# A two-layer cross-attention kernel: the first step of a turn's image probabilities set behind the next scores, and four row subtractions set one stop earlier

## The chip, the cores and the metric

The kernel runs on one core of one Trainium2 chip. The metric is the device time of one execution in microseconds (us), as the median of several runs. The engines are called as the profile calls them: PE is TensorE, the matrix engine (PEld is its weight load); DVE is VectorE, ACT is ScalarE, POOL is GpSimd; SPq is the queue on SyncE that issues nearly all DMAs.

## The reference

Two cross-attention layers run one after the other on `x` of shape (4, 512, 320), with 20 heads of width 16 and a context `ctx` of (4, 1024, 512). The last 4 tokens of the context are image tokens in layer 0; in layer 1 the first 77 are text and all others image tokens. Everything is float32.

```python
# layer 0
probs_t = softmax(q k_t^T * 0.25)                  # over 1020 text tokens
text_out = probs_t @ v_t
qsem = l2norm(probs_t @ text_ehs)                  # [.., 512] for each head and row
sem  = qsem @ l2norm(ip_ehs)^T
probs_ip = softmax(q k_ip^T * 0.25 + 0.5 * sem)    # over 4 image tokens
probs_ip = probs_ip * spatial_mask
x = (text_out + probs_ip @ v_ip) @ W_out + b_out + x
# layer 1
out_text = softmax(q k^T * 0.25) @ v               # over 77 tokens
out_ip   = softmax(q k_ip^T * 0.25) @ v_ip         # over the other 947
x = (out_text + out_ip) @ Wo.T + bo + x
```

## The kernel before

The rows of `x` are cut into 16 **turns** of 128 rows (4 batches, 4 turns each). Each turn has 5 **groups** of 4 heads, so the main loop runs over 80 groups `gi`. A group has two **units** (`i` = 0, 1) of two heads, and a unit four parts (`part0` to `part3`), which multiply probabilities with blocks of the context on PE (tiles `b` in PSUM, operands `xv`, `xs`, `xv_t`, `xs_t`; two of the products run on sums of blocks in the manner of Strassen and Winograd). After each part comes a **stop**; stops of a group are numbered `k` = 0 to 7. The stops hold the rest of the work:

- `item()` (stop 0 to 7, first thing) takes one piece from the queues `sub`, `late` and `proj`, in this order: a transpose for layer 1, small steps that finish layer 0's turn and start layer 1's, or a projection of the next batch.
- `fill0(gi + 1, k)` (stops 0 and 1) makes the next group's scores: 32 PE matmuls into two `sc` tiles of PSUM; ACT copies both to `e` (L490), DVE reduces both for the row maximum (`m<-sc`). There are two `sc` buffers in all, so the second fill's matmuls need the first fill's copies and reductions done. Layer 1's tiles `mx` and `ex` use the same two buffers.
- `l1_step()` (stops 2, 4, 5 and mostly 6) is a step of layer 1: maxima (`mx`, `m<-mx`, `nmz`), exponentials (`ex`, L551), and at stop 4 the values' product `pv`, which ACT copies to `pc` (L567). Its normalisation (`den`: a shuffle and a reciprocal on DVE, two products on POOL) is put at the end of `late` and mostly runs at stop 5.
- `max0(gi + 1)` (stop 2) transposes the row maxima, writes them to DRAM (`zd`) and reads them back broadcast over partitions (`bc`, 256 KB, L737).
- `end_stop(k)` (last thing of a stop) takes from `ew` the four pieces that `max0` put there. Each piece (`do_exp`) adds `bc`, the negated maximum of the row, to one `e` tile on DVE and takes ACT's exponential of it (L748). For half 0 the add is one instruction of 128x1024, and POOL then subtracts one block from another (L750); for half 1 it is a 128x768 add and a 128x256 `scalar_tensor_tensor` with `drop`. The order is unit 0 half 0, unit 0 half 1, unit 1 half 0, unit 1 half 1; below they are the first to fourth subtraction.

On POOL a unit also has its sum of blocks `s2` (L824), `e("11") + s2` (L843, needed by `part1`) and `e("12") - s2` (L845, needed by `part2`). `part0` ends with the DVE add `c<-b,p`, which needs ACT's copy `p` (L842); ACT then squares `c` (L828). `part1` lets DVE copy `p5` out of its tile (a row `p<-b`), and `part2` ends with the DVE adds `c<-b,u` and `c<-b,p`; the second of them reads the tile into which `part3` multiplies next.

After a turn's last group `finish(turn)` runs. `norms()` makes, on DVE, the reciprocal `r` of the sums, the squared norms `n` (five small instructions), `o` and `sem`, and on ACT `rn` (Ln and Exp). `exps()` is four small DVE instructions (`sem<-sem,rn`, `pe<-sem,ips`, `mx<-pe`, `pe<-pe,mx`) and an exponential on ACT (L910). It goes to `late` with five further steps, so that `item()` runs it at stop 0 of the next turn's first group, ahead of that stop's fill.

PE's and DVE's instructions are kept in the order in which the program records them. ACT's, POOL's and the DMA queues' are placed by the framework's scheduler.

Of the kernel before, what the change touches and what calls it, by code (L numbers as in the profile page):

```python
# [33 lines left out]
TURNS = [(b, s) for b in range(B) for s in range(ST)]  # L34
# [21 lines left out]
def xattn_pair(ctx_stack: ExitStack, tc: tile.TileContext, a: dict, out: bass.AP):  # L56
# [19 lines left out]
    def mm(out, lhsT, rhs, start, stop, on=False):  # L76
        tc.keep_in_program_order(nc.tensor.matmul(out, lhsT=lhsT, rhs=rhs, start=start, stop=stop, skip_group_check=on))  # L77
# [13 lines left out]
    def tr(out, in_, ident):  # L91
        tc.keep_in_program_order(nc.tensor.transpose(out, in_, ident))  # L92
# [11 lines left out]
    def tp(name):  # L104
        turn_of[0] += 1
        if tail[0]:
            return ps_tp.tile([P, 512], F32, tag="tp", name=name)
        if idle[0] and turn_of[0] % 4:
            return ps_qs.tile([P, 512], F32, tag=f"qs{turn_of[0] % 4 - 1}", name=name)
        return ps_tp.tile([P, 512], F32, tag="tp", name=name)  # L110
# [39 lines left out]
    def load_x(b, s, ns, pl, tag):  # L150
        t = pl.tile([P, ns, C], F32, tag=tag, name=f"{tag}_{b}_{s}")
        nc.sync.dma_start(t, a["x"][b, s * P : (s + ns) * P, :].rearrange("(t p) c -> p t c", p=P))
        return t
# [89 lines left out]
    def zero_below(t):  # L243
        nc.gpsimd.memset(t[64:, NC - 1, :], 0.0)
        return t
# [210 lines left out]
    late = deque()  # L456
# [3 lines left out]
    hold = [0]  # L460
    ready = {}
    pend = []
    ew = deque()

    def load_quad(l, z, turn, g):

        s = TURNS[turn][1]
        q = z.q1d[turn] if l else z.q0d[:, s * P : (s + 1) * P]
        k = buffer(l, turn, g)
        for r in range(4):  # L470
            c = 64 * g + D * r
            nc.sync.dma_start(qq[l][k][32 * r : 32 * r + D, :], q[c : c + D, :])
            nc.sync.dma_start(kq[l][k][32 * r : 32 * r + D, :], z.kd[l][c : c + D, :])
# [4 lines left out]
    def fill(c, m, name):  # L478


        ps = [ps_sc.tile([P, 2, 512], F32, tag="sc", name=f"sc{name}_{c}_{i}") for i in range(2)]
        for j in range(TH):
            t = (TH * c + j) * P
            for r in range(4):
                mm(ps[r // 2][:, r % 2, j * P : (j + 1) * P], kq[0][0][32 * r : 32 * r + D, t : t + P],
                   qq[0][0][32 * r : 32 * r + D, :], True, True)
        e = [ep.tile([P, 2, TH, P], F32, tag="e0", name=f"e{name}_{c}_{i}") for i in range(2)]

        for i in range(2):
            nc.scalar.copy(e[i].rearrange("p h t s -> p (h t s)"), ps[i].rearrange("p h n -> p (h n)"))  # L490
            j = 1 - i
            vec.tensor_reduce(m[:, c, 2 * j : 2 * j + 2, :],
                              ps[j][:, :, 0 : (TH - c) * P].rearrange("p h (t s) -> p h s t", s=P), AX.X, ALU.max)
        return e
# [185 lines left out]
    def l1_step():  # L680
        if stops[0] < hold[0]:
            return
        if l1:
            l1.popleft()()
        elif pend:
            pend.pop()()
# [14 lines left out]
    def fill0(gi, c):  # L701
        if gi >= len(G):
            return
        name = f"0_{gi}"
        if c == 0:
            ms[gi] = big.tile([P, 2, 4, P], F32, tag="m0", name=f"m{name}")
        e = fill(c, ms[gi], name)
        for i in range(2):
            es[gi, i, c] = e[i]
        if c:  # L710

            m = ms[gi]
            vec.tensor_tensor(m[:, 0], m[:, 0], m[:, 1], ALU.max)
            for i in range(2):
                x = m[:, 0, 2 * i : 2 * i + 2, :]
                vec.scalar_tensor_tensor(x, x, drop[:, 0:1], e[i][:, :, TH - 1, :], ALU.add, ALU.max)
            if gi + 1 < len(G):
                turn, g = G[gi + 1]
                load_quad(0, zs[TURNS[turn][0]], turn, g)
# [149 lines left out]
    def finish(turn):  # L869
        b, s = TURNS[turn]  # L870
        w, z, name = state.pop(turn), zs[b], f"0_{turn}"

        def small(tag, shape):
            return (st2 if tag in ("pT", "oT") else big).tile(shape, F32, tag=tag, name=f"{tag}_{name}")

        def wide(t, n=NIP):
            return t.unsqueeze(2).to_broadcast([P, H, n])

        z.xr[turn] = xr = load_x(b, s, 1, st3, "xr")
        nc.gpsimd.tensor_tensor(xr, xr, bo[0].unsqueeze(1).to_broadcast([P, 1, C]), ALU.add)  # L880
        pv, ss, ips = w["pv"], w["ss"], w["ips"]
        r = small("r", [P, H])
        o = small("o", [P, H, D])
        sem = small("sem", [P, H, NIP])
        n2 = small("n2", [P, H])
        rn = small("rn", [P, H])
        pe = small("pe", [P, H, NIP])
        mx = small("mx", [P, H])
        sums = small("sums", [P, H])
        re = small("re", [P, H])  # L890


        def norms():

            vec.reciprocal(r, pv[:, :, V0W - 1])
            vec.tensor_tensor(n2, ss[:, :, 0], ss[:, :, 1], ALU.add)
            vec.tensor_tensor(n2, n2, r, ALU.mult)
            vec.tensor_tensor(n2, n2, r, ALU.mult)
            vec.tensor_scalar(n2, n2, EPS2, None, ALU.max)
            nc.scalar.activation(rn, n2, AF.Ln)  # L900
            nc.scalar.activation(rn, rn, AF.Exp, scale=-0.5)
            vec.tensor_tensor(o, pv[:, :, 0:D], wide(r, D), ALU.mult)
            vec.tensor_tensor(sem, pv[:, :, D : D + NIP], wide(r), ALU.mult)

        def exps():
            vec.tensor_tensor(sem, sem, wide(rn), ALU.mult)
            vec.scalar_tensor_tensor(pe, sem, SEM_SCALE, ips, ALU.mult, ALU.add)
            vec.tensor_reduce(mx, pe, AX.X, ALU.max)
            vec.tensor_tensor(pe, pe, wide(mx), ALU.subtract)
            nc.scalar.activation(pe, pe, AF.Exp)  # L910

        def shares():
            vec.tensor_reduce(sums, pe, AX.X, ALU.add)
            vec.reciprocal(re, sums)
            vec.tensor_scalar(re, re, spat[:, s : s + 1], None, ALU.mult)
            vec.tensor_tensor(pe, pe, wide(re), ALU.mult)

        of2, box = o.rearrange("p h d -> p (h d)"), {}

        def turn_ip():  # L920
            pt = tp(f"pt_p_{name}")
            tr(pt[: H * NIP, 0:P], pe.rearrange("p h n -> p (h n)"), ident)
            box["pT"] = small("pT", [H * NIP, P])
            vec.tensor_copy(box["pT"], pt[: H * NIP, 0:P])

        def add_ip():
            pt = tp(f"pt_ip_{name}")
            mm(pt[:, 0:C], box["pT"], z.vip, True, True)
            vec.tensor_tensor(of2, pt[:, 0:C], of2, ALU.add)

        def turn_out():
            pt = tp(f"pt_o_{name}")
            for c, (c0, n) in enumerate(CK):
                tr(pt[:n, c * P : (c + 1) * P], of2[:, c0 : c0 + n], ident)
            box["oT"] = zero_below(small("oT", [P, NC, P]))
            vec.tensor_copy(box["oT"][:, 0:2].rearrange("p c s -> p (c s)"), pt[:, 0 : 2 * P])
            vec.tensor_copy(box["oT"][:64, 2, :], pt[:64, 2 * P : 3 * P])

        def multiply():
            pt = tp(f"pt_y_{name}")  # L940
            for c in range(NC):
                mm(pt[:, 0:C], box["oT"][:, c, :], wo0[:, c, :], c == 0, c == NC - 1)
            vec.tensor_tensor(xr[:, 0, :], pt[:, 0:C], xr[:, 0, :], ALU.add)
            layer1(turn)

        norms()
        late.extend([exps, shares, turn_ip, add_ip, turn_out, multiply])


    z, (turns, keys0, last_k, v0, vip, keys1, v1, q0) = projections(0)  # L950
# [55 lines left out]

    def end_stop(k):
        stops[0] += 1
        for _ in range({5: 2, 6: 1, 7: 1}.get(k, 0)):
            if ew:  # L1010
                ew.popleft()()

    def item():
        for q in (late,) if tail[0] and l1 else (sub, late, proj):
            if q:
                q.popleft()()
                break

    def stop(gi, k):

        item()
        if k < 2:
            fill0(gi + 1, k)
        if k in (2, 4, 5) or k == 6 and gi < len(G) - 2 or ending[0] and k < 2:
            l1_step()
        if k == 2:
            max0(gi + 1)
        end_stop(k)
# [65 lines left out]
```

## Time and profile before

| | |
|---|---|
| median of 3 runs | 3616.77 us (3614.4 to 3620.53) |
| the profiled execution's own time | 3614.53 us |
| its span, first to last instruction | 3612.8 us |
| mean granted PE clock | 0.973 of full speed |
| PE busy | 3496.2 us (97%) |
| PE's weight loads busy | 2787.8 us (77%) |
| DVE busy | 2101.1 us (58%) |
| ACT busy | 1471.5 us (41%) |
| POOL busy | 1021.5 us (28%) |

A row of the timeline reads: start in us from the span's start, duration in us, engine, source line, operation, tiles written and read, shape, count, and in brackets the idle time of the engine just before and what ended it. Rows of one kind that follow each other are merged. Most of DVE's instructions and all of PE's are recorded by helpers, so that they all stand at L87 and L77; the tiles tell them apart. An engine that is idle beside a busy PE costs nothing; what costs time is PE's own waiting, and PE's time at half clock.

### The profile page before, as it was taken

Reading aid. Unit: us, or ns where it says so; the run is one execution under the profiler, and the core shown is the slowest. Engines: PE = TensorE matmul, PEld = TensorE weight load, DVE = VectorE, ACT = ScalarE, POOL = GpSimd, SP = SyncE. Lnnn points to the kernel's source line nnn. Section 1 sums busy time; section 2 is a strip of 40 time slices with the busy share of each in tenths; the row PEclk is TensorE's granted clock in tenths of the full one; section 3 lists DMA queues with packets and bytes.
Section 4 is the critical chain, followed back from the end, with each engine's and each line's share of the span. In section 5 each row is a group of like instructions: output and inputs, shape, how many; then the busy total and the mean of one; then the engine's idle time right before and its main releaser. Section 6 shows DMA issues by size and latency. Waiting matters only on the chain.

```text
span 3612.8 us, 74199 instructions
## 1 busy us (share of the span) xinstructions
PE 3496.2 (97%) x29060; PEld 2787.8 (77%) x29060; DVE 2101.1 (58%) x3814; ACT 1471.5 (41%) x2807; POOL 1021.5 (28%) x1050
## 2 busy tenths in 40 slices
PE   7999999999999999999999999999999999999989
PEld 6777777777788777877777788777778777777766
DVE  2344555666655655566664655656666666666644
ACT  1333344444443443444443443444444444444422
POOL 2322222323332222233222232222323323332310
PEclk9999999999999999999999999999999999999976
DMA  6454332222344243222234434222232222222211
GB/s 210 107 130 118 96 67 41 44 42 55 81 98 114 56 103 97 56 52 41 58 78 112 97 83 102 57 60 44 48 84 49 46 45 52 43 47 42 47 31 32
DMA packets 700571, 258.76 MB, mean 72 GB/s; under 512 B 567952, under 2 KB 673904, under 8 KB 700224
## 3 DMA queue, kind: packets, MB, share of 16 engines
q1 hardware_dynamic: 699184, 250.42, 30.9%
q8 instruction: 232, 3.80, 0.5%
q0 software_dynamic: 864, 3.41, 0.4%
q14 instruction: 115, 0.94, 0.1%
q10 hardware_dynamic: 176, 0.20, 0.0%
HBM read 213.51 MB, written 40.33 MB: 70 GB/s over the span
## 4 chain that ended last, share of the span: by engine, by line
PE 85%; DVE 7%; ACT 3%; issue 2%; DMA 1%; SPq 1%; POOL 0%; POOLq 0%; ACTq 0%; DVEq 0%
PE b L77 50%; PE ex L77 6%; PE pv L77 5%; PE mx L77 4%; PE sc L77 4%; PE pt_k L77 4%; PE pt_v L77 4%; DVE e L87 4%; PE pt_y L77 2%; PE pt_q L77 2%; ACT e L490 2%; DVE m L87 1%; PE mx L92 1%; ACT e L748 1%; ACT junk L828 1%
## 5 line engine op out<-in xcount | busy, mean ns | idle before, releaser
L77 PE MATMUL b<-xv_t,e 128*128 128x277 f32 x2560 | 662.3, 401 | 1.7 <-DVE c L87 1.6
L77 PE MATMUL b<-xv,e 128*128 128x277 f32 (+1 forms) x2560 | 649.4, 406 | 2.8 <-ACT e L748 2.8
L77 PEld LDWEIGHTS b<-xv,e 128*128 128x128 f32 x2560 | 478.7, 189 | 134.7 <-ACT e L748 3.4
L77 PEld LDWEIGHTS b<-xv_t,e 128*128 128x128 f32 x2560 | 476.2, 191 | 108.7 <-DVE c L87 4.0
L748 ACT ACTIVATE e<-e 128x1024 f32<-128x1024 f32 x320 | 338.2, 1057 | 462.9 <-DVE e L87 462.8
L843 POOL TENSOR_TENSOR e<-e,s 128x512 f32<-128x512 f32 x160 | 224.0, 1400 | 982.5 <-PE b L77 982.4
L87 DVE TENSOR_REDUCE m<-mx 128x2 f32<-128x870 f32 (+3 forms) x345 | 366.7, 1066 | 115.4 <-PE ex L77 92.2
L87 DVE TENSOR_REDUCE m<-sc 128x256 f32<-128x1024 f32 (+1 forms) x320 | 343.3, 1088 | 135.4 <-PE sc L77 119.1
L551 ACT ACTIVATE e<-ex 128x1024 f32<-128x1024 f32 x320 | 325.7, 1019 | 209.0 <-PE ex L77 208.0
L490 ACT COPY e<-sc 128x1024 f32<-128x1024 f32 x320 | 320.4, 1010 | 177.6 <-PE sc L77 150.5
L77 PE MATMUL mx<-kq,qq 16*128 16x512 f32 x1280 | 380.2, 668 | 6.3 <-DMA qq<-q1d 4.0
L77 PE MATMUL ex<-qa,kq 19*128 19x128 f32 x5120 | 382.2, 291 | 3.8 <-DVE qa L87 3.1
L87 DVE TENSOR_TENSOR e<-e,bc 128x1024 f32<-128x1024 f32 x320 | 369.8, 1177 | 2.2 <-DMA bc<-zd 2.2
L750 POOL TENSOR_TENSOR e<-e 128x512 f32<-128x512 f32 x160 | 205.7, 1285 | 571.2 <-ACT e L748 567.1
L87 DVE TENSOR_TENSOR c<-b,p 128x256 f32<-128x256 f32 x320 | 134.1, 419 | 389.2 <-PE b L77 341.0
L828 ACT ACTIVATE junk<-c 128x256 f32<-128x256 f32 x480 | 198.6, 414 | 395.7 <-DVE c L87 391.2
L77 PEld LDWEIGHTS ex<-qa,kq 19*128 19x128 f32 x5120 | 324.5, 194 | 16.9 <-issue 6.3
L77 PE MATMUL b<-xs,e 128*128 128x256 f32 x1280 | 335.1, 407 | 0.0
L77 PE MATMUL b<-xs_t,e 128*128 128x256 f32 x1280 | 320.0, 393 | 4.3 <-POOL e L843 4.3
L77 PE MATMUL b<-xs_t,s 128*128 128x256 f32 x1280 | 302.7, 379 | 0.0
L77 PEld LDWEIGHTS b<-xs,e 128*128 128x128 f32 x1280 | 240.7, 198 | 48.8 <-issue 2.1
L77 PEld LDWEIGHTS b<-xs_t,e 128*128 128x128 f32 x1280 | 231.5, 190 | 55.4 <-issue 13.9
(190 smaller groups left out, 4173.6 us busy)
## 6 DMA issues: line engine op xcount, KB each, us to landing
kq<-kd SPq DMA_DIRECT2D x640, 64.0 KB
v1q<-v1d SPq DMA_DIRECT2D x80, 373.5 KB
bc<-zd SPq DMA_DIRECT2D x80, 256.0 KB
xv<-v0d SPq DMA_DIRECT2D x480, 42.0 KB
xv_t<-v0d SPq DMA_DIRECT2D x320, 42.0 KB
L_xattn_W_k<-in_L_xattn_W_k_dram SPq DMA_DIRECT2D x13, 640.0 KB
L_xattn_Wv_ip<-in_L_xattn_Wv_ip_dram SPq DMA_DIRECT2D x13, 640.0 KB
raw<-in_ctx_dram SPq DMA_DIRECT2D x32, 256.0 KB
```

Of the source, the lines that this page charges most:

```text
L77: tc.keep_in_program_order(nc.tensor.matmul(out, lhsT=lhsT, rhs=rhs, start=start, stop=stop, skip_group_check=on))
L87: return lambda *args, **kw: keep(getattr(self.engine, name)(*args, **kw))
L92: tc.keep_in_program_order(nc.tensor.transpose(out, in_, ident))
L490: nc.scalar.copy(e[i].rearrange("p h t s -> p (h t s)"), ps[i].rearrange("p h n -> p (h n)"))
L551: nc.scalar.activation(e.rearrange("p i j s -> p (i j s)"), ps.rearrange("p i n -> p (i n)"), AF.Exp)
L748: nc.scalar.activation(flat, flat, AF.Exp)
L750: nc.gpsimd.tensor_tensor(e[:, 1], e[:, 1], e[:, 0], ALU.subtract)
L828: nc.scalar.activation(junk, x, AF.Square, accum_out=self.w["ss"][:, self.h + r, k : k + 1])
L843: nc.gpsimd.tensor_tensor(self.e("11"), self.e("11"), self.s2, ALU.add)
```

## The change

Two edits:

1. `exps()` no longer goes to `late`. It is kept in a queue `after`, and at stop 0 of the next turn's first group it runs behind `fill0` in place of that stop's `item()`; the five further steps are put into `late` when it has run. The last turn is as before.
2. `end_stop` takes the four subtractions at stops 4 (one), 5 (two) and 6 (one), where it took them at stops 5 (two), 6 (one) and 7 (one).

```diff
+    after = deque()
     ew = deque()
...
         norms()
-        late.extend([exps, shares, turn_ip, add_ip, turn_out, multiply])
+
+        def exps_and_on():
+            exps()
+            late.extend([shares, turn_ip, add_ip, turn_out, multiply])
+
+        (after if turn + 1 < len(TURNS) else late).append(exps_and_on)
...
     def end_stop(k):
         stops[0] += 1
-        for _ in range({5: 2, 6: 1, 7: 1}.get(k, 0)):
+        for _ in range({4: 1, 5: 2, 6: 1}.get(k, 0)):
             if ew:
                 ew.popleft()()
...
     def stop(gi, k):
 
-        item()
+        behind = k == 0 and after
+        if not behind:
+            item()
         if k < 2:
             fill0(gi + 1, k)
+        if behind:
+            after.popleft()()
         if k in (2, 4, 5) or k == 6 and gi < len(G) - 2 or ending[0] and k < 2:
             l1_step()
```

In the built program PE's instructions stand in the same order as before, and SPq's too but for two pairs of neighbours. On DVE, ACT and POOL no instruction is added or left out; those of the subtractions, of `exps()` and what the scheduler placed around them have moved. On POOL the second unit's `s2` now mostly stands ahead of the first unit's L843. On ACT the fourth exponential stands ahead of the square of the last product (L828 of `b`), the turn's first two copies L490 ahead of L910, and the first exponential ahead of the copy `pc` except in a turn's second group.

## The prediction

> **What bounds the kernel now.** I read the page first: PE is busy for 97% of the span, and the chain that ended last is PE for 85%, so only PE's own waits and its clock can give time. Next the waits of PE (engine, line and tile, releaser: us in total, times, longest):
>
> ```profile
> PE sc L77 <- ACT e L490: 47.9, 31, 3.2
> ...
> PE b L77 <- POOL e L843: 4.3, 6, 1.4
> ...
> PE b L77 <- DVE c L87: 1.6, 4, 0.6
> ```
>
> The second fill of a group waits for ACT's copies of the first; nothing else in the main loop is near it. The timeline shows these 31 waits: ten of 3.16 to 3.20 us and five of 0.33 to 1.62 in first groups of turns 1 to 15, sixteen of 0.74 in other groups (31.7 + 4.3 + 11.9 = 47.9). The timeline of the change from turn 10 to 11 shows where one comes from (the turn's first unit starts at 2488.71):
>
> ```profile
> 2490.94 1.67 DVE L87 TENSOR_TENSOR e<-e,bc 128x768 f32<-128x768 f32 x1
> 2492.54 1.48 DVE L87 SCALAR_TENSOR_TENSOR e<-e,drop,bc 128x256 f32<-128x256 f32 x1
> 2496.69 1.19 DVE L87 SCALAR_TENSOR_TENSOR pe<-sem,ips 128x80 f32<-128x80 f32 x1
> 2498.45 0.27 ACT L910 ACTIVATE pe<-pe 128x80 f32<-128x80 f32 x1 [1.96 <-DVE pe L87]
> 2498.63 2.03 ACT L490 COPY e<-sc 128x1024 f32<-128x1024 f32 x2
> 2500.71 1.39 PE L77 MATMUL sc<-qq,kq 16*128 16x128 f32 x32 [3.16 <-ACT e L490]
> 2502.03 3.54 PE L77 MATMUL b<-xs,e 128*128 128x256 f32 x8
> ```
>
> The fourth subtraction runs into the new group, the norms and `exps()` queue behind it, and ACT's copies wait behind L910 although the first fill ended at 2493.85. The last row is a second cost: eight matmuls that take 1.99 us elsewhere take 3.54. The windows of first units tell why (PE, PEld, DVE, ACT, POOL busy, granted clock, DMA share, GB/s):
>
> ```profile
> 1420.50:1439.70 19.20, 17.58 (x147) 13.99 (x146) 17.95 (x37) 8.71 (x18) 4.72 (x4) 1.00 0.27 56
> 2488.70:2511.20 22.50, 19.34 (x148) 15.12 (x146) 18.09 (x37) 10.01 (x20) 5.73 (x4) 0.92 0.17 30
> 3272.10:3296.00 23.90, 20.74 (x148) 16.30 (x146) 18.11 (x37) 10.01 (x20) 5.73 (x4) 0.86 0.16 28
> ```
>
> After a wait of 3.16 the clock is halved for a while: 0.08 of 22.5 is 1.8 us lost, 0.14 of 23.9 is 3.3. Over the ten long waits the windows give 22.5 us, and 1.7 more after one of the two waits of 1.6 (turn 5's); turn 6's, the first row, left the clock whole. So the prize is 47.9 + 24.2 us.
>
> **The change part by part.** No instruction is added; adds (1.13 for 128x1024, 0.95 for 128x768, 0.48 for the rest), exponentials (1.06) and POOL's passes (1.27) move, and no DMA does.
>
> *Plain groups.* In the group at 2570.99 the fourth add now starts where the third did, at 2570.42, ends with its rest at 2571.8, and its exponential at 2572.9. Copy `p` follows the square (0.55) at 2573.5, `c` starts when PE's second product ends (2575.02), and with the fill over at 2576.13 ACT copies until 2578.2 and DVE reduces until 2578.7. PE wants the buffers at 2579.79: the 0.74 is gone with 1.1 to spare. On POOL `s2` now stands ahead of L843: 2573.0 to 2574.3, L843 to 2575.5, wanted at 2576.07. Gain 16 x 0.74 = 11.9 (0 to 11.9).
>
> *Turns 1, 5, 6, 9, 10.* Projections stretch the old turn's last unit (26.6 us for 18.8 in the last four), so the fourth subtraction at stop 6 and the norms behind it end early. Their sc waits go: 3.2 + 1.1, 1.7 of clock, and 0.8 twice for L843 in turns 9 and 10. Gain 7.6.
>
> *The ten other turn changes.* Here earlier is not simply better. The fourth add takes the third's place, 0.57 us ahead of the new group, so its exponential ends 1.95 us into it (1.43 + 1.06 and a step); POOL runs `s2`, L843 and L845 back to back until about 5.9 (3 x 1.27), and the norms, behind the square of 0.55, start at 2.6, right beside them. The nearest row is turn 6's, where the old order already gave this meeting (its unit starts at 1420.55):
>
> ```profile
> 1422.87 1.28 POOL L843 TENSOR_TENSOR e<-e,s 128x512 f32<-128x512 f32 x1 [1.38 <-PE b L77]
> 1422.95 2.45 DVE L87 TENSOR_TENSOR n<-n,r 128x20 f32<-128x20 f32 x2
> 1425.32 1.28 POOL L845 TENSOR_TENSOR e<-e,s 128x512 f32<-128x512 f32 x1
> 1425.44 1.19 DVE L87 TENSOR_SCALAR n<-n 128x20 f32<-128x20 f32 x1
> 1430.96 1.39 PE L77 MATMUL sc<-qq,kq 16*128 16x128 f32 x32 [1.62 <-ACT e L490]
> ```
>
> Instructions of 0.18 take 1.2: each lets one POOL pass by. So `n` is ready at 6.1, as there; `rn` (2 x 0.22), `p` (0.37), `c` (0.42) and the square follow, and ACT's copies, no longer behind L910, run from 8.0 or 8.3 to 10.0 or 10.3; PE wants the buffer at 8.85. A wait of 1.1 to 1.45 remains, and 0.1 where `p5`, now behind `exps()`, is late: I take 1.3, so 31.7 - 13 = 18.7 is gained. [...] Waits of 1.6 halved the clock once in two; for 1.3 I let a third of the 22.5 stay: gain 15 (0 to 22.5).
>
> [...]
>
> *New waits.* The first subtraction at stop 4 waits for `bc` on DVE. Behind it there stand `p5`, `den`, the next maxima, the second and third subtraction, and `c`, for which PE's `part3` waits; on ACT, `pc` behind its exponential. The timeline of the unit that starts at 2589.34:
>
> ```profile
> 2593.70 0.34 SPq L737 DMA_DIRECT2D bc<-zd  x1
> 2594.77 1.05 DVE L87 TENSOR_REDUCE m<-mx 128x2 f32<-128x870 f32 x1
> 2598.57 0.42 DVE L87 COPY p<-b 128x256 f32<-128x256 f32 x1 [2.75 <-PE b L77]
> 2605.33 0.41 DVE L87 TENSOR_TENSOR c<-b,p 128x256 f32<-128x256 f32 x1
> 2606.19 2.13 PE L77 MATMUL b<-xv_t,e 128*128 128x277 f32 x8
> ...
> 628.63 1.23 DVE L87 TENSOR_TENSOR e<-e,bc 128x1024 f32<-128x1024 f32 x1 [1.66 <-DMA bc<-zd]
> ```
>
> The last row's `bc` was issued at 625.10: 3.53 us from issue to use. DVE has 2.75 us free in front of `p5`, enough for the 1.13 as a rule. With the add starting at s, `pc` ends at s + 2.6 (exponential 1.25 after the add's start, 1.06, copy 0.37); the shuffle stood at 2598.92, the chain behind it has 0.25 of idle time in front of `nmz` and 0.45 between `c` and `part3`. So PE waits for what s exceeds 2598.92 + 0.70 - 2.6, which is 7.7 us after the unit's start. Here s = 2593.70 + 3.53, 7.9: a wait of 0.2. In most of the 33 units without projections `bc` is issued 3.1 to 3.5 us after the start, s is about 6.8, and nothing is late; five come to 0.2 to 0.5. In a turn's second group `bc` is issued at 5.3 to 6.4, `pc` is ahead of the exponential, the add and `p5` (1.13 + 0.42) alone stand before the shuffle and the point is 8.8: four units wait 0.6 to 1.1, the five and the four together 5 to 6 us. With an unclear 4 us in the first turns: cost 10 (0 to 30).
>
> Sum: 11.9 + 7.6 + 18.7 + 15 - 10 = 43 us. The profiled execution took 3614.5 (span 3612.8 and 1.7 around it), 2.3 below the median of 3616.8. From the median: 3574; range of this case 3560 to 3588.
>
> **Rivals.**
> - *Everything goes.* DVE and POOL do not meet at the turn change, no wait is left, `bc` is in time: 3616.8 - 47.9 - 24.2 - 1.6 = 3543. For it: turns 9 and 10 ran their norms in 0.18 steps. Against: the row of 2.45. Chance 0.2.
> - *The meeting eats the turn changes.* The ten waits stay at 3.2 with their half clock: 11.9 + 7.6 - 10 gives 3607. For it: at 2495.96 to 2497.88 two small DVE instructions already lost 1.4 us to POOL. Against: turn 6's 1.62. Chance 0.13.
> - *Slower: `bc` is late everywhere.* If s is 10 in all 33 units (it is 9.8 in the one at 3139.59), PE waits 2.3 each, 76 us, and half of the waits halve the clock, 28 more; against a gain of 53: 3668. It decides from s = 9.3 on (33 x 1.6 = 53). For it: the first use was 7 to 12 us after the issue nearly everywhere, so the trace seldom tested this. Against: 3.53 where it did. Chance 0.09.
> - *No difference* (3609.5 to 3624): the second rival with costs toward 30, or ACT's copies as late as before because DVE's reductions, needed too, end late. That the edit does nothing is excluded by the order of the built program. Chance 0.08.
>
> **How the numbers follow.** Forecast 0.5, rivals 0.2, 0.13, 0.09, 0.08. A measurement of this kernel can tell 0.2%, 7.2 us, from no change. Faster: 0.5 + 0.2 + 0.13 = 0.83; same 0.08; slower 0.09. The range takes in the forecast and the first two rivals: 3541 to 3608.
>
> **What would show it.** In the profile of the changed kernel: the 0.74 waits are absent; `sc <- ACT e L490` falls from 47.9 to about 13; `n<-n,r` shows 1.2 us at the ten turn changes; their windows mostly have a clock of 1.00; `e<-e,bc` waits for `bc` in second groups, and `b <- DVE c` grows to 5 to 15 us. A wait for `c` or `p5` in most units would make the prediction wrong on the slow side, norms of 0.18 on the fast side.

## The result, and the profile after

The changed kernel takes 3555.5 us (median of 4 runs, 3548.9 to 3559.2), the kernel before 3617.7 (median of 4, 3614.4 to 3620.5): a ratio of 0.9826, with a 95% interval of 0.9808 to 0.9845, so faster by 1.7%. The profiled execution took 3559.2 us, its span is 3557.5 and its mean granted clock 0.978.

The waits of PE (engine, line and tile, releaser: us in total, times, longest; the patch moves the lines down by one, so L490 is now L491 and L843 is L844):

```profile
PE b L77 <- DVE c L87: 11.1, 15, 1.5
PE sc L77 <- ACT e L491: 8.4, 10, 1.0
...
PE b L77 <- DVE p L87: 2.7, 8, 1.0
...
PE b L77 <- POOL e L844: 1.3, 2, 0.8
```

The wait for ACT's copies fell from 47.9 to 8.4 us. The sixteen of 0.74 us are gone; ten are left, one at each of the ten turn changes, nine of 0.82 and one of 0.98. The wait for `c` grew from 1.6 to 11.1. All of PE's idle time fell from 113.3 to 81.7 us.

The timeline of the change from turn 10 to 11, whose first unit starts at 2456.54:

```profile
2459.77 1.27 POOL L844 TENSOR_TENSOR e<-e,s 128x512 f32<-128x512 f32 x1
2459.89 2.41 DVE L87 TENSOR_TENSOR n<-n,r 128x20 f32<-128x20 f32 x2
2462.54 0.22 ACT L901 ACTIVATE rn<-n 128x20 f32<-128x20 f32 x1 [3.77 <-DVE n L87]
2464.20 1.91 ACT L491 COPY e<-sc 128x1024 f32<-128x1024 f32 x2
2466.16 1.51 PE L77 MATMUL sc<-qq,kq 16*128 16x128 f32 x32 [0.82 <-ACT e L491]
2467.90 1.97 PE L77 MATMUL b<-xs,e 128*128 128x256 f32 x8 [0.23 <-DVE p L87]
```

The small products `n<-n,r` take 1.2 us each beside POOL's passes. ACT's copies, no longer behind the exponential of `pe`, start 7.66 us into the unit, where they started at 9.92. The windows of first units (unit's length, then PE, PEld, DVE, ACT, POOL busy, granted clock, DMA share, GB/s):

```profile
2456.50:2475.60 19.10, 17.86 (x147) 14.08 (x146) 16.27 (x36) 8.85 (x19) 3.72 (x3) 1.00 0.19 34
2838.50:2858.90 20.40, 19.34 (x148) 15.19 (x146) 16.39 (x36) 8.96 (x19) 3.72 (x3) 0.92 0.18 33
```

Six of the ten have a clock of 1.00, four have 0.92 (the second row is one of these).

Where the time went is best seen by units (a unit starts with its first 128x298 product; us summed from those starts; turn 0 is left out):

| profiled execution | first units, ten turn changes | first units, turns 1, 5, 6, 9, 10 | first units of the 60 other groups | second units | span |
|---|---|---|---|---|---|
| before | 230.7 | 96.1 | 1204.2 | 1582.1 | 3612.8 |
| changed | 199.0 | 86.7 | 1178.8 | 1595.4 | 3557.5 |
| edit 1 alone | 199.9 | 92.1 | 1205.2 | 1582.1 | 3573.4 |
| edit 2 alone | 212.9 | 87.1 | 1179.0 | 1593.3 | 3575.6 |
| two subtractions each at stops 5 and 6 | 200.4 | 86.7 | 1200.4 | 1580.6 | 3568.1 |
| POOL's passes left out at turn changes | 174.5 | 86.7 | 1179.2 | 1592.6 | 3522.3 |
| norms late, steps kept | 184.4 | 92.3 | 1178.1 | 1592.8 | 3548.4 |
| three subtractions at stop 5 in second groups | 193.5 | 86.7 | 1194.4 | 1592.8 | 3563.8 |
| norms late where they meet POOL | 182.4 | 86.3 | 1179.1 | 1593.9 | 3537.2 |

From before to changed: 31.7 and 9.4 and 25.4 us less, 13.3 more in second units, and 2.1 less elsewhere make the 55.3 of the spans.

### The profile page after: what moved, and what is told of

The parts are those of the page before. It is cut to its first block, busy times and chain, and to the rows that moved or that the text cites. A ratio compares the mean times of both kernels' runs of the same rounds, so it can differ in the third digit from the quotient of the medians.

```text
span 3557.5 us, 74109 instructions
## 1 busy us (share of the span) xinstructions
PE 3472.5 (98%) x29060; PEld 2767.5 (78%) x29060; DVE 2056.3 (58%) x3814; ACT 1478.0 (42%) x2807; POOL 992.8 (28%) x1050
## 4 chain that ended last, share of the span: by engine, by line
PE 85%; DVE 8%; DMA 3%; issue 2%; SPq 1%; ACT 1%; POOL 0%; DVEq 0%; POOLq 0%; ACTq 0%
PE b L77 51%; PE ex L77 6%; PE sc L77 4%; PE pv L77 4%; PE pt_k L77 4%; PE pt_v L77 4%; PE mx L77 4%; PE pt_y L77 2%; DVE m L87 2%; PE pt_q L77 2%; DVE e L87 2%; DMA bc<-zd 2%; PE mx L92 1%; DVE den L87 1%; DVE n L87 1%
## 5 line engine op out<-in xcount | busy, mean ns | idle before, releaser
L77 PE MATMUL b<-xv_t,e 128*128 128x277 f32 x2560 | 661.2, 401 | 11.5 <-DVE c L87 11.1
L844 POOL TENSOR_TENSOR e<-e,s 128x512 f32<-128x512 f32 x160 | 203.1, 1269 | 1033.2 <-PE b L77 1033.0
L491 ACT COPY e<-sc 128x1024 f32<-128x1024 f32 x320 | 322.8, 1012 | 175.0 <-PE sc L77 134.0
L87 DVE TENSOR_TENSOR e<-e,bc 128x1024 f32<-128x1024 f32 x320 | 355.2, 1110 | 59.0 <-DMA bc<-zd 58.3
L825 POOL TENSOR_TENSOR s<-e,e 128x512 f32<-128x512 f32 x160 | 204.4, 1278 | 472.5 <-ACT e L749 305.3
L77 PE MATMUL b<-xs,e 128*128 128x256 f32 x1280 | 323.3, 396 | 3.4 <-DVE p L87 2.7
L751 POOL TENSOR_TENSOR e<-e 128x512 f32<-128x512 f32 x160 | 209.3, 1308 | 377.1 <-ACT e L749 377.1
L77 PEld LDWEIGHTS b<-xs,e 128*128 128x128 f32 x1280 | 233.4, 192 | 49.5 <-issue 6.2
```

What stands on the lines that cost most here:

```text
L87: return lambda *args, **kw: keep(getattr(self.engine, name)(*args, **kw))
L751: nc.gpsimd.tensor_tensor(e[:, 1], e[:, 1], e[:, 0], ALU.subtract)
L825: nc.gpsimd.tensor_tensor(self.s2, self.e("21"), self.e("22"), ALU.add)
L844: nc.gpsimd.tensor_tensor(self.e("11"), self.e("11"), self.s2, ALU.add)
```

## The experiments

The diffs are against the changed kernel, and only their main lines are shown.

### Edit 1 alone

```diff
-        for _ in range({4: 1, 5: 2, 6: 1}.get(k, 0)):
+        for _ in range({5: 2, 6: 1, 7: 1}.get(k, 0)):
```

> Only exps() is put behind the fill; the four subtractions stay at stops 5 (two), 6 and 7. Theory (each edit has its own prize, and at the ten turn changes both are needed): ACT's copies no longer stand behind L910, so the ten waits of 3.2 us become about 1.0 to 1.6, and most of the half clock behind them goes; the sixteen waits of 0.74 us stay, and the rows DVE waits for bc and PE waits for c stay near those of before (c 1.6 us). Ten times 2 us and some 15 us of clock: about 3582 us. Rival (the fourth subtraction, which runs into the new group, holds DVE and with it norms and copies): the ten waits stay near 3 us and the time near 3617. Second rival (exps() was nearly all of it): the ten waits vanish, about 3570 us.

Measured: 3578.2 us median, ratio 0.9893 (0.9876 to 0.9909). The time is near the theory's 3582, with waits of 0.82 us (one of 0.66) at the ten turn changes where it had 1.0 to 1.6. But that both edits are needed there did not hold, as the table shows. The timeline of the same turn change (the unit starts at 2468.22), and the wait in all:

```profile
2473.79 0.39 DVE L87 TENSOR_TENSOR n<-n,r 128x20 f32<-128x20 f32 x2
...
2475.92 1.91 ACT L491 COPY e<-sc 128x1024 f32<-128x1024 f32 x2
```

```profile
PE sc L77 <- ACT e L491: 21.3, 28, 0.8
```

The norms stand behind the fourth subtraction, start 2.2 us later than in the changed kernel (5.57 us into the unit, not 3.35), and run in steps of 0.2 us between two of POOL's passes. So the copies start 7.70 us into the unit, as in the changed kernel (7.66), and PE waits the same 0.82. Edit 1 alone gives 30.8 of the 31.7 us of the turn changes.

### Edit 2 alone

```diff
-        (after if turn + 1 < len(TURNS) else late).append(exps_and_on)
+        late.extend([exps, shares, turn_ip, add_ip, turn_out, multiply])
...
-        behind = k == 0 and after
-        if not behind:
-            item()
+        item()
...
-        if behind:
-            after.popleft()()
```

> Only the subtractions are moved to stops 4 (one), 5 (two) and 6 (one); exps() stays ahead of the fill. Theory: the sixteen waits of 0.74 us vanish (18 us with what follows them), turns 1, 5, 6, 9 and 10 give their 9 us, the new waits for c cost some 13 us as in the changed kernel, and the ten turn changes look like turn 6's of before: a wait of about 1.6 us, with the clock halved behind some of them. 18 + 9 + 7 - 13 + 10 times 1.6 + about 10 of clock: about 3571 us. Rival (the place of exps() decides the turn changes): the ten waits stay near 3.2 us with their half clock, 3597 us.

Measured: 3562.4 us median (3556.8 to 3577.3), ratio 0.9855 (0.983 to 0.9879). The profiled execution is the longest of the four, at a clock of 0.975, so its 212.9 us at the turn changes are too many for the median. The waits themselves tell more: ten of 1.75 to 1.92 us, 17.7 in all. The other columns of the table are within some 2 us of the changed kernel's. The rival with waits of 3.2 is out. Alone the edits give 38 and 54 us, together 62: at the turn changes both take away parts of the same wait, and beside edit 1, edit 2 saves only 0.9 us there.

### POOL's passes left out at the turn changes

```diff
+            bare = self.i == 0 and self.gi > 0 and self.gi % HG == 0
-            nc.gpsimd.tensor_tensor(self.e("11"), self.e("11"), self.s2, ALU.add)
+            if not bare:
+                nc.gpsimd.tensor_tensor(self.e("11"), self.e("11"), self.s2, ALU.add)
...
-            nc.gpsimd.tensor_tensor(self.e("12"), self.e("12"), self.s2, ALU.subtract)
+            if not bare:
+                nc.gpsimd.tensor_tensor(self.e("12"), self.e("12"), self.s2, ALU.subtract)
```

> The changed kernel without POOL's two passes e("11") + s2 and e("12") - s2 in the first unit of every turn but the first, which leaves that part of the computation out there. Theory (DVE's small norms instructions alternate with POOL's passes): without the passes n<-n,r takes 0.18 us instead of 1.2, n is ready some 3 us earlier, the ten waits of 0.82 us and the half clock behind four of them go: 18 us less than the changed kernel, about 3538 us. Rival (ACT's own order or the chain of rn sets the copies' start): n<-n,r is short but the ten waits of about 0.8 us stay, 3550 to 3556 us.

Measured: 3526.0 us median, ratio 0.9753 (0.9736 to 0.9769). The same turn change (start 2441.86):

```profile
2445.21 0.39 DVE L87 TENSOR_TENSOR n<-n,r 128x20 f32<-128x20 f32 x2
...
2447.50 1.93 ACT L491 COPY e<-sc 128x1024 f32<-128x1024 f32 x2
```

The norms are short, the copies start 5.64 us into the unit, and no wait for them is left. What is left of the meeting in the changed kernel costs 24.5 us in the ten units (199.0 to 174.5), more than the 18 that the theory allowed: 12.4 us of idle time, 6.7 of half clock, and 5.4 by which rows behind the waits are slower (the fill takes 1.51 us there and 1.17 here). An instruction `n<-n,r` took 1.19 us beside a pass of POOL's in the changed kernel and takes 0.18 here, without one.

### Two subtractions each at stops 5 and 6

```diff
-        for _ in range({4: 1, 5: 2, 6: 1}.get(k, 0)):
+        for _ in range({5: 2, 6: 2}.get(k, 0)):
```

> The changed kernel with the subtractions at stops 5 (two) and 6 (two). Theory: the new waits were the price of stop 4, where bc may not have come: DVE's wait for bc falls from 58 us to under 5 and PE's wait for c from 11.1 to about 2, which gives 13 us back; but the fourth subtraction stands 1.1 us later behind the third one, so at the ten turn changes the wait for the copies grows from 0.82 to between 1.3 and 1.9 us with more half clock (8 to 20 us), and the plain groups keep almost no margin: 3545 to 3565 us. [...]

Measured: 3569.3 us median, ratio 0.9866 (0.9852 to 0.9881). The waits of PE:

```profile
PE b L77 <- POOL e L844: 24.7, 43, 2.0
PE sc L77 <- ACT e L491: 5.6, 9, 0.6
...
PE b L77 <- DVE c L87: 1.6, 4, 0.6
```

That `c` waits because of stop 4 is right: 11.1 became 1.6, and DVE's wait for `bc` 58.3 became 2.2. But the time is above the theory's 3545 to 3565, as the price turned up in a place that the theory had not named. The fourth exponential ends 1.2 us later (3.06 us into group 62's first unit, for one, not 1.88), and POOL's pass L751 ends there at 3.09; `s2` follows both, and L844, which stands behind `s2` on POOL, is late in 43 groups. At the turn changes the wait for the copies shrank to 0.62 instead of growing, as the wait of 0.61 for L844 comes first.

### Three subtractions at stop 5 in second groups

```diff
-        for _ in range({4: 1, 5: 2, 6: 1}.get(k, 0)):
+        for _ in range(({5: 3, 6: 1} if gi % HG == 1 else {4: 1, 5: 2, 6: 1}).get(k, 0)):
```

> The changed kernel, and only in a turn's second groups, where bc is issued latest, the subtractions at stops 5 (three) and 6 (one). Theory (the price of stop 4 is paid there): PE's wait for c falls from 11.1 to about 4 us, DVE's wait for bc from 58 to about 40, and the second units of second groups fall by 8 to 10 us together: about 3547 us. Rival (three subtractions, 3.7 us of DVE in one piece, come too late for c or layer 1's maxima at stop 6): the same units wait as long or longer, 3553 to 3565 us.

Measured: 3566.8 us median, ratio 0.9864 (0.9828 to 0.9901): the rival, a little above its 3553 to 3565. The waits of PE:

```profile
PE b L77 <- DVE c L87: 11.2, 22, 0.9
PE b L77 <- POOL e L844: 6.3, 9, 0.8
```

DVE's wait for `bc` fell to 19.7 us, but the waits for `c` only became shorter and more, since three subtractions in a row hold `c` themselves (in group 61 `c` starts where the third ends, and PE waits 0.67). The larger loss was named by neither theory nor rival: the third groups' first units rose by 14.4 us, with L844 late in seven of them by 0.7. So the stop that waits for `bc` is dear, and both other places that I tried are dearer.

### Norms late, in three attempts

> The whole computation. norms() too is put behind the fill of stop 0, in the place that the changed kernel gives to exps(), and exps() becomes the item of stop 1. Theory (the meeting of the norms' small DVE instructions with POOL's passes held the copies): the norms run after POOL's passes, n<-n,r takes 0.2 us, the ten waits for the copies of 0.82 us go, and the ten first units fall from 19.9 us to 17.3, as with the passes left out: 26 us less than the changed kernel, about 3530 us. Limit: the norms are 1.9 us of DVE where exps() was 1.0, ahead of the copy p5; if PE waits for p5 up to 1 us ten times, and each such wait costs twice its length, 3550. Rival (the passes' absence itself was the gain, by less traffic of POOL): the ten units stay near 19.9 us and the time near 3555.

> The whole computation. norms() is the item of stop 1 of the new turn's first group, behind the copy p5, and exps() the item of stop 2. Theory: as for the norms behind the fill of stop 0, and p5 is not delayed, so the ten first units come to 17.3 us: about 3527 us. The second fill's reductions on DVE start up to 1 us later, which costs nothing if the row maxima have that much to spare, and up to 10 us if bc then comes late. Rival: the norms make the second fill's reductions and with them bc late at ten turn changes: DVE's wait for bc grows by 10 us and PE waits for c, 3540 to 3550.

The edit of the first of the two (the second puts `norms` itself into `late`, ahead of `exps`):

```diff
-        norms()
...
+        rest = [exps, shares, turn_ip, add_ip, turn_out, multiply]
...
+        def norms_and_on():
+            norms()
+            late.extend(rest)
...
+            after.append(norms_and_on)
```

Measured: 3598.6 and 3636.9 us, ratios 0.9946 (0.993 to 0.9963) and 1.0057 (1.0034 to 1.008). Neither theory nor rival had this. The waits for the copies are gone in both and `n<-n,r` takes 0.18. But each kernel takes every later step of the turn one or two stops later, layer 1 with them. The timeline of a step of layer 1 in the changed kernel, and then of the first of these two:

```profile
2593.03 0.27 PE L92 MATMUL pt_nm<-ident,nmz 128*128 128x128 f32 x1
...
2597.14 0.70 PE L77 MATMUL mx<-kq,qq 16*128 16x512 f32 x2
2597.16 0.71 PE L77 MATMUL ex<-qa,kq 19*128 19x128 f32 x8
...
2597.68 0.59 PE L77 MATMUL mx<-kq,qq 16*128 16x512 f32 x2
2597.71 0.61 PE L77 MATMUL ex<-qa,kq 19*128 19x128 f32 x8
```

```profile
2633.22 0.27 PE L92 MATMUL pt_nm<-ident,nmz 128*128 128x128 f32 x1
2633.42 1.13 PE L77 MATMUL mx<-kq,qq 16*128 16x512 f32 x4
...
2633.97 1.16 PE L77 MATMUL ex<-qa,kq 19*128 19x128 f32 x16
```

The transpose `pt_nm` now stands right ahead of the step that needs its result `qa`, so `ex` starts 0.55 us behind `mx` where the two ran side by side. This is so in some 60 of layer 1's steps, where it was in four. The time in which PE works on `mx` or `ex` (the union of all their records) grew from 426.0 to 462.5 us, and PE's idle time by 10.0 (L844 is late again, 18.1 us in 23 units, and three waits for layer 1's keys `kq`, 14.3 us, are new, while other waits went): 46.5 of the 48.4 us by which the span grew. In the second kernel the union is 463.6, and PE waits 25.0 us for the next batch's weights (`pt_v`) where it waited 6.7.

> The kernel with norms() at stop 1, and the subtractions at stops 5 (three) and 6 (one), so that none stands where bc may not have come, and the fourth stays where the change put it. Theory: DVE's wait for bc falls to under 5 us and PE's wait for c from 9 to 11 us to about 2; the second units fall by the 13 us that the change added to them: about 3514 us. Rival (three subtractions in one piece, 3.7 us of DVE, make c or the maxima of layer 1 at stop 6 late): PE waits for c or p5 in most of the 80 groups by 0.3 to 1 us, 3540 to 3600 us.

> The kernel with norms() at stop 1, and only in a turn's second groups, where bc is issued latest, the subtractions at stops 5 (three) and 6 (one). Theory: the waits for c in second groups (four to six of 1.1 to 1.5 us) go, the small ones in other groups stay: PE's wait for c falls from about 9 us to about 3, 8 us less than with norms() at stop 1 alone, about 3519 us. Rival (three in one piece are too late): second groups wait for c or p5 as before or longer, 3527 to 3540 us.

Measured: 3636.0 and 3635.9 us (ratios 1.0065 and 1.0051), beside 3636.9 without their edit of the stops. They tell nothing on stop 4: with the steps shifted PE waits for `c` only 1.8 us in all without them.

The third attempt keeps every other step at its stop:

```diff
-            vec.tensor_tensor(o, pv[:, :, 0:D], wide(r, D), ALU.mult)
...
+            vec.tensor_tensor(o, pv[:, :, 0:D], wide(r, D), ALU.mult)
...
-        norms()
...
+        def exps_and_shares():
+            exps()
+            shares()
+
+        def norms_and_on():
+            norms()
+            late.extend([exps_and_shares, turn_ip, add_ip, turn_out, multiply])
```

> The whole computation. norms() stands behind the fill of stop 0 as before, but exps() and shares() are one item at stop 1 and the product o is made in the item of stop 2, so that all other steps stay at the stops where the changed kernel has them; PE's, POOL's and the DMA queue's order are the changed kernel's. Theory (the two kernels with late norms were slow because every later step, layer 1's and the projections' too, came one or two stops later): the ten first units fall from 19.9 us to 17.3 to 18.0 with n<-n,r at 0.2 us, all other groups stay as in the changed kernel: 3526 to 3535 us. Rival (late norms themselves are bad, by p5 or by the row maxima of the next group coming late): PE waits for p5 or for bc and c in the turns' first groups, 3555 us or more.

> The late norms with the other steps kept, and three subtractions at stop 5 in a turn's second groups. Theory: the two act in different units and add: 25 us and 8 us less than the changed kernel, about 3521 us. Rival: one of the two is lost as described for it alone, 3530 to 3555 us.

Measured: 3549.5 us, ratio 0.9806 (0.9772 to 0.9839), and with three subtractions at stop 5 in second groups 3561.4, ratio 0.9842 (0.9808 to 0.9875). That the shifted steps were the cause is shown: with them kept, `mx` and `ex` take 426.1 us again, the time is 49 us below the first attempt's, and the turn changes take 184.4 us for 199.0. The forecast of 3526 to 3535 is missed, by a wait that takes the old one's place:

```profile
PE mx L92 <- DVE pT L87: 13.2, 14, 2.0
```

With `norms()`, `exps()` and `shares()` close together on DVE, its copy `pT` comes too late for PE's transposes of the next row maxima: by 0.87 us in the first units of turns 3 to 15, which are nine of the ten turn changes and turns 5, 6, 9 and 10, and by 1.97 in turn 1's. Turns 1, 5, 6, 9 and 10, which had no meeting, lose 5.6 us. Which of the three pieces is to blame was not separated. The kernel with both edits loses 12 us to the one with late norms alone, as the three subtractions lost 11 to the changed kernel.

### Norms late only where they meet POOL

```diff
-            vec.tensor_copy(box["pT"], pt[: H * NIP, 0:P])
+            nc.scalar.copy(box["pT"], pt[: H * NIP, 0:P])
...
+        elif turn + 1 in (1, 5, 6, 9, 10):
+            norms()
+            after.append(exps_and_on)
+        else:
+            after.append(norms_and_on)
```

> The whole computation. The late norms with the other steps kept, but only at the ten turn changes where they met POOL's passes (turns 1, 5, 6, 9 and 10 stay as in the changed kernel), and the copy pT, which PE's transposes of the next row maxima waited for by 0.87 us, goes from DVE to ACT, where it stands behind the fill's last copy. Theory: the ten first units fall from 18.4 us, with the norms late alone, to 17.3 to 17.6, turns 1, 5, 6, 9 and 10 come back to 86.7 us together, and PE's wait for pT goes from 13.2 us to under 3: some 10 and 6 us less than the kernel with the norms late alone, or 24 less than the changed kernel's profile: 3528 to 3537 us, close to the kernel with POOL's passes left out. Rival (the row maxima themselves are late, so that the transposes wait for m where they waited for pT): the ten units stay near 18.2 us, 3540 to 3546 us.

Measured: 3540.7 us median of 5 (3538.9 to 3542.6), ratio 0.979 (0.9776 to 0.9805): faster than before by 2.1% and below the changed kernel (0.9808 to 0.9845), by some 15 us. The timeline (start 2447.85):

```profile
2461.69 0.26 ACT L924 COPY pT<-pt_p 80x128 f32<-80x128 f32 x1 [0.38 <-PE pt_p L92]
...
2465.91 0.30 PE L92 MATMUL pt_nm<-ident,nmz 128*128 128x128 f32 x1 [0.35 <-DVE ips L87]
```

ACT copies `pT` in time, and turns 1, 5, 6, 9 and 10 are back at 86.3 us. But a wait of 0.35 us for DVE's copy `ips` follows in nine of the ten units: they come to 18.2 us, not 17.3. That is the rival's length and time, though the transposes do not wait for the row maxima `m`, as it had it; the waits in these units, 0.35 and some 0.08 for `c`, are half of the 0.9 that is missing, and the rest was not traced.

## Why the prediction was right, and where its sum was off

**The mechanism.** Nearly every step is in the profile: no wait of 0.74, `n<-n,r` at 1.2 us in the ten turn changes, `n` ready late, a short wait left for the copies, most windows at full clock, and `c` late behind `bc`. The time alone would not tell it: 3555.5 lies 18.5 us under the forecast of 3574, 4.5 under the range given for this case, and nearer to the 3543 of the first rival, whose mechanism is not in the profile.

**The sum.** 62 us were gained, 43 forecast. 6.9 of the 19 are no term of the sum: the forecast took its 43 off the median, but the profiled execution of before lies 3.2 below its median of 3617.7, and that of the changed kernel is the longest of its runs, 3.7 above. Profile against profile 55.3 stand against 43:

| term | forecast | measured |
|---|---|---|
| sixteen plain groups | 11.9 | 18.5 |
| turns 1, 5, 6, 9, 10 | 7.6 | 9.4 |
| ten turn changes, waits and clock | 33.7 | 31.7 |
| new waits (second units) | -10 | -13.3 |
| other first units and the rest | 0 | 9.0 |

- *Plain groups* are the term that was mis-sized. The unit went from 18.35 to 17.19 us, so a wait of 0.74 cost 1.16: the fill behind it takes 1.51 us and not 1.17. "16 x 0.74" counted the idle time alone.
- *Turn changes.* The wait is 0.82, not 1.3, as the copies start at 7.66 and not at 8.0 to 8.3. The half clock that stays is 0.08 of four windows of 20.4 to 22.0 us, 6.7 us, where a third of 22.5, 7.5, was let stay. By these two the ten units should have gained 31.7 - 8.4 and 22.5 - 6.7, 39.1 us in all, and they gained 31.7: 3.1 us of other short waits (for `p` and `pT`) are new, and the fill behind the wait takes 1.51 us. That the term came out so near its forecast is in part luck, as errors cancelled.
- *New waits.* 13.3 for 10. Five units wait 0.35 to 0.56, near the forecast's 0.2 to 0.5; but six second groups wait 1.02 to 1.47, where four of 0.6 to 1.1 were forecast. The point at which the waits start was right, as this second group shows (its second unit starts at 2516.55):

```profile
2522.52 0.34 SPq L738 DMA_DIRECT2D bc<-zd  x1
2526.57 1.23 DVE L87 TENSOR_TENSOR e<-e,bc 128x1024 f32<-128x1024 f32 x1 [3.53 <-DMA bc<-zd]
...
2534.70 2.13 PE L77 MATMUL b<-xv_t,e 128*128 128x277 f32 x8 [1.22 <-DVE c L87]
```

The subtraction starts 10.0 us into the unit; the point for second groups was 8.8, and PE waits 1.22. Only the 3.53 us from issue to use was short: it is 4.05 here, and 3.4 to 4.6 in the units of groups like this one.

- *The rest.* 6.4 of the 9.0 are one unit (in group 42) where the execution before happened to wait 2.93 us for weights, at half clock behind it. No edit touches it.

**The rivals.** That everything goes needed norms of 0.18; they take 1.19, and leaving POOL's passes out shows what it would have been: 3526. That the meeting eats the turn changes is refuted by 0.82 for 3.16. That `bc` is late everywhere is refuted too: DVE waits for it 40 times, 58.3 us, but `c` keeps PE waiting in 15 units only, four of them as before.

**What the working missed.** It took the gain of the turn changes for the work of both edits together. Edit 1 alone lets the copies start as early (7.70 us for 7.66): the later norms miss POOL's passes, the earlier ones meet them.

## What to carry to other kernels

A short wait of the bound engine can cost more than its idle time (here 0.74 us cost 1.16): price it by the unit's length with and without it, not by the wait. When a piece of work is moved out of a meeting, keep every later step at its place; here late norms lost 43 us against the changed kernel with the later steps shifted by a stop, and won 15 with them kept, at the ten places that needed it and with one copy moved to ACT. And a stop earlier trades one wait for another (here PE's waits for the copies fell from 47.9 to 8.4 us, and those for `c` grew from 1.6 to 11.1): follow the moved instruction's own inputs (`bc`) and what stands behind it (`c`, `s2`, L844) at each candidate place.

## What the runs showed of the hardware

- An idle microsecond of PE mostly cost more than one, at no fixed price. Against the kernel before, idle time fell by 31.6 us and the span by 55.3 in the changed kernel, by 22.0 and 39.4 with edit 1 alone, by 28.1 and 37.2 with edit 2 alone, by 48.8 and 90.5 without POOL's passes, and by 41.5 and 75.6 in the last kernel. From the changed kernel to three subtractions at stop 5 in second groups idle time rose by 7.2 us and the span by 6.3. In single units at full clock it depends on what stands behind the wait: 0.74 ahead of the fill cost 1.16, as said, but 0.59 ahead of the product that needs L844 cost 0.66 (two subtractions each at stops 5 and 6, group 62: 17.86 us for 17.20). Why the fill is slower behind a wait stays open.
- Even waits of 0.82 us, with one of about 0.2 behind them, were followed by a half clock in four of ten turn changes (a granted clock of 0.92 over the unit, 1.00 in the six others), and in five with edit 1 alone (0.92 over the unit shown above). With three subtractions at stop 5 in second groups the same ten units with nearly the same waits (8.4 and 8.3 us) take 193.5 us for 199.0, near the 192.3 that are left of 199.0 without its 6.7 us of half clock. In stretches of 1 us the granted clock behind such a wait reads 0.50 (2850.47 to 2852.47 in the changed kernel). What decides whether it follows, no run shows.
- `mx` and `ex` take 1.2 us side by side (2597.14 to 2598.32 in the changed kernel) and 1.7 when `ex` starts 0.55 us later (2633.42 to 2635.13 in the first kernel with late norms).
